# The product G v of a twelve-layer linear attention kernel: from one float32 product to three float32r passes of 128 columns

## The chip, the cores and the metric

The kernel runs on one core of a Trainium2 chip. The metric is the device time of one execution in microseconds. The engines are called as the profile calls them: PE is TensorE (PEld its weight loads), DVE is VectorE, ACT is ScalarE, POOL is GpSimd and SP is SyncE, which issues transfers here.

## What is computed

Twelve layers of attention without a softmax over 16 sequences of 256 tokens with 128 features, in 16 heads of 8 features, then a residual sum, a layer norm, a gated feed-forward network of 384 hidden features, and a second residual sum and layer norm. Cut to what matters:

```python
for i in range(12):
    qkv = x @ Wqkv[i].T + bqkv[i]
    q, k, v = jnp.split(qkv, 3, axis=-1)          # each (16, 256, 128), then split in 16 heads
    att = jnp.einsum('bhqd,bhkd->bhqk', q, k) * scale
    y = jnp.einsum('bhqk,bhkd->bhqd', att, v)
    x = y @ Wproj[i].T + bproj[i] + x
x = layernorm(x0 + x)
x = layernorm(x + ((silu(x @ wg.T) * (x @ wu.T)) @ wd.T))
```

## The kernel before

Since there is no softmax, q (k^T v) can be taken in any order, and the kernel never forms the tokens of the inner layers. It keeps for each sequence an affine map t (`tst`, 128 x 130: a 128 x 128 matrix and a column for the offset) that takes the tokens of the input to those of the layer. With the centred Gram matrix G of the input tokens, 128 x 128 for each sequence (`g0`), a layer needs per head only the small product k^T (G v), where k and v stand for the maps times the weights.

The 16 sequences are worked on in eight pairs (PB = 2), and the pairs in two sets of four (G = 4, NO = 2), half a layer apart. The steps of one layer are:

1. `products` for each pair. From the second layer on: k and v of both sequences into one PSUM bank by `mm_kv` (L439 to L441: three float32r passes of 256 columns a sequence, high and low halves of the map times high and low halves of the weights, without low times low), a copy of the bank's 512 columns to `kv` in SBUF, then q by `mm_q` (L447 to L449: three float32r passes of 260 columns a pair), its copy to the q part of `qgv`, and G v by `mm_gv` (L460: one float32 product of 128 columns for each sequence, from `g0` and the v part of `kv`), and its copy to the last part of `qgv`. In the first layer v is the raw weight itself, and k and q come from raw weights too.
2. `heads` for each set: the small products of k and G v of all heads by `mm_m` (L504), the sum with an offset term (L514) and a mask, then y by `mm_y` (L522).
3. `projection` for each pair: a high half of y (copy, ACT or DVE), a low half (subtraction on DVE, L535), three passes of 260 columns by `mm_w` (L539 to L541), the sum into `tst` (DVE, L546), and new halves of the map, `thl`: the high one on ACT (L204, a copy helper), the low one on POOL (L209, a subtraction helper).

Ahead of the layers, `prologue` makes the Gram matrices of a pair (L341) and takes off the mean on DVE, which writes `g0` (L358). Behind them, `ffn` works through the eight pairs; its pair p overlaps the last layer where there is room. Its high and low halves of the hidden features lie in tiles `hh0`, `hh1`, `hl0` and `hl1`, one group for each pair, 512 float32r columns each.

The order of instructions on each engine is written by a planner, `Plan`. Each operation has its costs on the engines that may do it, what it reads and writes, and a priority (the layer, plus half a layer for the second set, plus small amounts such as QLATE = 0.3 for q). `Plan.run` keeps a clock for each engine and takes again and again, among the operations that could start first, the one with the lowest priority number. Where an operation may run on ACT or DVE, the one that would end earlier gets it. The planner's clock is an estimate; on the chip the order alone stands, and semaphores make an engine wait. PSUM has eight banks, which the planner hands out (`Val("bank")`).

The planner's costs that bear on the change are the following:

```python
def mm32(n=C):
    return max(220, 4 * n / 2.4 + 8)
def mmr(n):
    return max(111, 0.447 * n + 5)
```

Of the kernel before, what the change touches and what calls it, by code (L numbers as in the profile page):

```python
# [9 lines left out]
F32 = mybir.dt.float32  # L10
F32R = mybir.dt.float32r
# [3 lines left out]
ALU = mybir.AluOpType  # L15
# [6 lines left out]
C = 128  # L22
# [3 lines left out]
PB = 2  # L26
NP = B // PB
# [6 lines left out]
NB = 2  # L34
# [38 lines left out]
PE, ACT, DVE, POOL, SP = "pe", "act", "dve", "pool", "sp"  # L73
# [92 lines left out]
# [8 lines that stand above are left out]
def act(n, sbuf=False, pointers=0):  # L174
    return (94 if sbuf else 51) + 93 * pointers + n / 1.2


def dve(n, fast=False):
    return 69 + n / (1.92 if fast else 0.96)


def pool(n):
    return 147 + 2.1 * n


def flat(t):
    return t.rearrange("p a b -> p (a b)")
# [3 lines left out]
def linear_attention_ffn_kernel(ctx: ExitStack, tc: tile.TileContext, x, xt, wall, wq0, bias, wg, wu, wd, out):  # L191
    nc = tc.nc
# [3 lines left out]
    new = lambda name, shape, dt=F32: sb.tile([128, *shape], dt, name=name)  # L196

    plan = Plan({"bank": 8, "raw": RAW, "weights": WSLOTS, "turned": WSLOTS})
    banks = [ps.tile([128, 512], F32, name=f"bank{i}") for i in range(8)]
    bank = lambda v: banks[v.slot]  # L200

    def copy(e, dst, src):
        if e == ACT:
            nc.scalar.copy(dst, src)  # L204
        else:
            (nc.vector if e == DVE else nc.gpsimd).tensor_copy(dst, src)  # L206
# [71 lines left out]
    wraw = [new(f"wraw{i}", [4 * C]) for i in range(RAW)]  # L278
# [40 lines left out]
    thl = [new(f"thl{p}", [2, PB, W], F32R) for p in range(NP)]  # L319
    means = new("means", [B])  # L320
    g0 = [new(f"g0_{p}", [PB, C]) for p in range(NP)]
    kvs = [new(f"kv{p}", [PB, 2, C]) for p in range(NP)]
    qss = [t[:, : PB * W].rearrange("p (a b) -> p a b", b=W) for t in qgvs]
    gvs = [t[:, PB * W :].rearrange("p (a b) -> p a b", b=C) for t in qgvs]
    yhl = [new(f"yhl{p}", [2, PB * W], F32R) for p in range(NP)]
    named = lambda: [Val() for _ in range(NP)]
    vt, vc, vhi, vlo, vm, vg0, vkv, vyh, vyl, vqo, vw = (named() for _ in range(11))

    nmeans, tmeans = new("nmeans", [B]), new("tmeans", [B])

# [92 lines left out]
    def products(l, p, prio):  # L423

        raw, whv, _ = wts[l]
        bs = slice(p * PB, (p + 1) * PB)
        hl = lambda i, s, n=1: whl[whv.slot][:, i, s * C : (s + n) * C]
        hi, lo = thl[p][:, 0], thl[p][:, 1]
        kv, qs, gv = kvs[p], qss[p], gvs[p]
        if l == 0:  # L430
            tv = lambda b: wraw[raw.slot][:, 2 * C : 3 * C]
            src = raw
        else:
            pkv, pq = Val("bank"), Val("bank")

            def mm_kv(e):
                for b in range(PB):
                    o = bank(pkv)[:, b * 2 * C : (b + 1) * 2 * C]
                    nc.tensor.matmul(o, hi[:, b, 0:C], hl(0, 1, 2), start=True, stop=False)  # L439
                    nc.tensor.matmul(o, hi[:, b, 0:C], hl(1, 1, 2), start=False, stop=False)  # L440
                    nc.tensor.matmul(o, lo[:, b, 0:C], hl(0, 1, 2), start=False, stop=True)  # L441
            plan.op({PE: 6 * mmr(256)}, mm_kv, [vhi[p], vlo[p], whv], [pkv], prio)
            plan.op({ACT: act(512), DVE: dve(512)}, lambda e: copy(e, kv.rearrange("p a b c -> p (a b c)"), bank(pkv)), [pkv], [vkv[p]], prio)

            def mm_q(e):
                o = bank(pq)[:, : PB * W]
                nc.tensor.matmul(o, hl(0, 0), flat(hi), start=True, stop=False)  # L447
                nc.tensor.matmul(o, hl(0, 0), flat(lo), start=False, stop=False)  # L448
                nc.tensor.matmul(o, hl(1, 0), flat(hi), start=False, stop=True)  # L449
            plan.op({PE: 3 * mmr(PB * W)}, mm_q, [vhi[p], vlo[p], whv], [pq], prio + QLATE)  # L450
            q = lambda: bank(pq)[:, : PB * W].rearrange("p (b w) -> p b w", w=W)
            plan.op({ACT: act(PB * C), DVE: dve(PB * C)}, lambda e: copy(e, qs[:, :, 0:C], q()[:, :, 0:C]), [pq], [vq[p]], prio + QLATE)
            plan.op({DVE: 130}, lambda e: nc.vector.tensor_scalar(qs[:, :, C], q()[:, :, C], bcol[:, l, 0:1], None, ALU.add), [pq, vbias], [vqo[p]], prio + QLATE)  # L453
            tv = lambda b: kv[:, b, 1, :]
            src = vkv[p]
        pgv = Val("bank")

        def mm_gv(e):
            for b in range(PB):
                nc.tensor.matmul(bank(pgv)[:, b * C : (b + 1) * C], g0[p][:, b, :], tv(b), start=True, stop=True)  # L460
        plan.op({PE: 2 * mm32()}, mm_gv, [vg0[p], src], [pgv], prio)
        plan.op({ACT: act(256), DVE: dve(256)}, lambda e: copy(e, flat(gv), bank(pgv)[:, : PB * C]), [pgv], [vgv[p]], prio)
        if l == L - 1:

            def rest(e):
                copy(e, tst[:, bs, 0:C], center.unsqueeze(1).to_broadcast([128, PB, C]))
                copy(e, tst[:, bs, C], mb[:, bs])
            plan.op({ACT: act(PB * C, True) + 100, DVE: dve(PB * C, True) + 75}, rest, [vhi[p], vlo[p], vmb], [vt[p], vc[p]], prio)
# [90 lines left out]
    for t in cps:  # L559
        nc.gpsimd.memset(t, 0.0)  # L560
    for p in range(NP):
        t = {f"{n}{j}": new(f"{n}{j}_{p}", [512], F32R) for n in ("hh", "hl") for j in range(NB)}
        t.update({
            "tt": qgvs[p][:, PB * W : PB * W + 2 * C], "x1": kvs[p].rearrange("p a b c -> p (a b c)"), "sg0": xts[p], "sg1": qgvs[p][:, :512],
            "xh": flat(yhl[p])[:, :512], "xl": thl[p].rearrange("p a b c -> p (a b c)")[:, :512],
            "ve": new(f"ve{p}", [4]), "rs": new(f"rs{p}", [4]), "nb": new(f"nb{p}", [4]), "nm": new(f"nm{p}", [4]), "st": new(f"st{p}", [K, 3]),
            "cr": new(f"crow{p}", [PB]), "cp": cps[p % 2], "cq": cqs[p % 2],
        })
        ctxs.append(t)
# [147 lines left out]
    for l in range(L):  # L717
        if l + 1 < L:
            prep_weights(l + 1)
        for o in range(NO):  # L720
            at = l + OSTEP * o
            for p in range(o * G, (o + 1) * G):
                products(l, p, at)
            for r, py in enumerate(heads(l, o, at, [(l, o)] * (l < OWN) + [(l + o, 1 - o)] * (OWN <= l + o < L))):
                projection(l, o * G + r, py, at + (LSTEP * r if l == L - 1 else 0))
        if l < NP:
            center_tokens(l, l + 2)
# [35 lines left out]
```

## Time and profile before

| what | value |
|---|---|
| median of three runs | 309.67 us (308.54 to 309.88) |
| time of the profiled execution | 309.26 us |
| span of the profiled execution, first to last instruction | 307.2 us |
| PE, PEld busy | 297.3 us (97%), 272.3 us (89%) |
| DVE, ACT, POOL busy | 227.2 (74%), 221.3 (72%), 136.4 us (44%) |
| mean granted TensorE clock | 0.989 |
| G v, layers two to twelve | 352 instructions for 176 products, from 27.8 to about 236 us |

The busy time of an engine is the union of its instructions' times. TensorE's matmuls are pipelined: one starts well before the one ahead of it has ended, so what each takes of the engine is read from the distance between starts, and not from its length. A float32 product of TensorE appears as two instructions, each with a weight load, and a float32r pass as one with one load. The shapes of float32r operands are shown as f32 in TensorE's rows.

### The profile page before, as it was taken

The page shows a single profiled execution, that of the slowest core. Times are in us where ns is not written, and L with a number is a line of the kernel's source. Part 1 is how long each engine was busy: PE and PEld are TensorE (multiplying, and loading weights), DVE is VectorE, ACT ScalarE, POOL GpSimd, SP SyncE. Part 2 cuts the span into 40 slices and gives each one's busy share as a digit, 9 for nine tenths or more (in the row PEclk, how much of TensorE's full clock was granted, in tenths as well). Part 3 has the DMA queues.
Part 4 walks back from the last instruction along what each step waited for, and adds up shares of the span by engine and source line. Part 5 has one row for each costly group of instructions (what it writes and reads, how often), then busy time and mean ns, then how long its engine had stood idle before and what let it go on. Part 6 is the DMA issues. An engine that isn't in the chain of part 4 may idle for free.

```text
span 307.2 us, 12904 instructions
## 1 busy us (share of the span) xinstructions
PE 297.3 (97%) x5384; PEld 272.3 (89%) x5384; DVE 227.2 (74%) x680; ACT 221.3 (72%) x571; POOL 136.4 (44%) x234
## 2 busy tenths in 40 slices
PE   8999999999999999999999999999999999999971
PEld 8989999999999999999999999999999988888840
DVE  3797887777677676776767877787554699899993
ACT  2547877867768677777677666776986768968964
POOL 6246353334541345314453144521442456568582
PEclk9999999999999999999999999999999999999995
DMA  7534213122031120311202112130000000000214
GB/s 211 149 99 128 71 39 89 35 55 71 9 82 38 42 84 2 90 37 43 82 4 53 38 28 55 30 81 2 4 2 3 2 1 2 0 0 22 83 34 137
DMA packets 22489, 15.65 MB, mean 51 GB/s; under 512 B 1952, under 2 KB 19872, under 8 KB 22432
## 3 DMA queue, kind: packets, MB, share of 16 engines
q1 hardware_dynamic: 21872, 14.62, 17.5%
q8 instruction: 42, 0.69, 0.9%
q10 hardware_dynamic: 560, 0.22, 0.3%
q14 instruction: 15, 0.12, 0.1%
HBM read 8.02 MB, written 2.10 MB: 33 GB/s over the span
## 4 chain that ended last, share of the span: by engine, by line
PE 88%; DVE 7%; ACT 3%; issue 1%; POOLq 0%; POOL 0%
PE bank L460 14%; PE bank L439 8%; PE bank L522 8%; PE bank L441 7%; PE bank L440 7%; PE bank L447 5%; PE bank L504 5%; PE bank L541 4%; PE bank L539 4%; PE bank L540 4%; PE bank L448 3%; PE bank L449 3%; PE bank L341 3%; PE bank L665 2%; PE bank L681 2%; PE bank L682 2%
## 5 line engine op out<-in xcount | busy, mean ns | idle before, releaser
L209 POOL TENSOR_TENSOR thl<-tst,thl 128x260 fp32r<-128x260 f32 x88 | 64.5, 764 | 122.9 <-ACT thl L204 122.9
L204 ACT COPY qgv<-bank 128x256 f32<-128x256 f32 x171 | 60.8, 376 | 20.5 <-PE bank L449 13.5
L204 ACT COPY kv<-bank 128x512 f32<-128x512 f32 (+1 forms) x93 | 53.3, 575 | 18.6 <-PE bank L441 13.4
L439 PE MATMUL bank<-whl,thl 128*128 128x256 f32 x176 | 51.8, 294 | 0.0
L441 PE MATMUL bank<-whl,thl 128*128 128x256 f32 x176 | 49.6, 282 | 0.0
L440 PE MATMUL bank<-whl,thl 128*128 128x256 f32 x176 | 49.4, 281 | 0.0
L460 PE MATMUL bank<-kv,g 128*128 128x128 f32 x352 | 46.0, 275 | 0.0
L546 DVE TENSOR_TENSOR tst<-bank,tst 128x260 f32<-128x260 f32 x96 | 36.9, 425 | 11.9 <-PE bank L541 9.1
L204 ACT CAST thl<-tst 128x260 fp32r<-128x260 f32 x88 | 33.0, 408 | 14.6 <-DVE tst L546 14.5
L460 PEld LDWEIGHTS bank<-kv,g 128*128 128x128 f32 x352 | 42.7, 191 | 0.4 <-issue 0.4
L453 DVE TENSOR_SCALAR qgv<-bank,bcol 128x2 f32<-128x2 f32 x88 | 19.3, 221 | 27.6 <-ACT qgv L204 23.0
L439 PEld LDWEIGHTS bank<-whl,thl 128*128 128x128 f32 x176 | 33.1, 188 | 4.1 <-issue 4.0
L535 DVE TENSOR_TENSOR yhl<-bank,yhl 128x260 fp32r<-128x260 f32 x96 | 34.3, 421 | 2.4 <-ACT yhl L204 2.4
L440 PEld LDWEIGHTS bank<-whl,thl 128*128 128x128 f32 x176 | 33.2, 189 | 0.0
L441 PEld LDWEIGHTS bank<-whl,thl 128*128 128x128 f32 x176 | 33.1, 188 | 0.0
L447 PE MATMUL bank<-thl,whl 128*128 128x260 f32 x88 | 29.0, 329 | 0.0
L522 PE MATMUL bank<-qgv,gm 32*32 32x130 f32 x1536 | 25.9, 280 | 0.2 <-DVE gm L212 0.2
L204 ACT CAST yhl<-bank 128x260 fp32r<-128x260 f32 (+1 forms) x61 | 22.3, 418 | 5.2 <-PE bank L522 3.8
L206 DVE CAST yhl<-bank 128x260 fp32r<-128x260 f32 x43 | 16.5, 424 | 11.8 <-PE bank L522 11.8
L448 PE MATMUL bank<-thl,whl 128*128 128x260 f32 x88 | 24.8, 282 | 0.0
L449 PE MATMUL bank<-thl,whl 128*128 128x260 f32 x88 | 24.7, 281 | 0.0
L522 PEld LDWEIGHTS bank<-qgv,gm 32*32 32x32 f32 x1536 | 17.3, 103 | 5.6 <-ACT kv L204 0.3
(153 smaller groups left out, 705.8 us busy)
## 6 DMA issues: line engine op xcount, KB each, us to landing
wraw<-wall SPq DMA_DIRECT2D x12, 256.0 KB, 3.0
wpt<-whl SPq DMA_DIRECT2D x24, 96.0 KB, 2.2
qgv<-x SPq DMA_DIRECT2D x8, 256.0 KB, 5.4
xt<-xt SPq DMA_DIRECT2D x8, 256.0 KB, 3.3
out<-kv SPq DMA_DIRECT2D x7, 256.0 KB, 2.3
wpt<-whl SPq DMA_DIRECT2D x24, 64.0 KB, 2.6
wpt<-whl SPq DMA_DIRECT2D x24, 32.0 KB, 1.9
wraw<-wg SPq DMA_DIRECT2D x1, 192.0 KB, 3.4
```

The source lines that it names most:

```text
L204: nc.scalar.copy(dst, src)
L209: (nc.vector if e == DVE else nc.gpsimd).tensor_tensor(dst, a, b, ALU.subtract)
L439: nc.tensor.matmul(o, hi[:, b, 0:C], hl(0, 1, 2), start=True, stop=False)
L440: nc.tensor.matmul(o, hi[:, b, 0:C], hl(1, 1, 2), start=False, stop=False)
L441: nc.tensor.matmul(o, lo[:, b, 0:C], hl(0, 1, 2), start=False, stop=True)
L447: nc.tensor.matmul(o, hl(0, 0), flat(hi), start=True, stop=False)
L448: nc.tensor.matmul(o, hl(0, 0), flat(lo), start=False, stop=False)
L449: nc.tensor.matmul(o, hl(1, 0), flat(hi), start=False, stop=True)
L460: nc.tensor.matmul(bank(pgv)[:, b * C : (b + 1) * C], g0[p][:, b, :], tv(b), start=True, stop=True)
L522: nc.tensor.matmul(bank(pys[r])[group(g + r), b * W : (b + 1) * W], gm[group(g), r * PB + b, :], qss[p][group(g), b, :], start=True, stop= ...
L535: plan.op({DVE: dve(PB * W)}, lambda e: nc.vector.tensor_tensor(yl, bank(py)[:, : PB * W], yh.bitcast(F32), ALU.subtract), [py, vyh[p]], [ ...
L546: plan.op({DVE: dve(PB * W)}, lambda e: nc.vector.tensor_tensor(ts, bank(pw)[:, : PB * W], ts, ALU.add), [pw], [vt[p], vc[p]], prio)
```

## The change

From the second layer on, `mm_gv` computes G v of each sequence in three float32r passes of 128 columns that add up in PSUM: high G times high v, high G times low v, low G times high v. The first layer keeps its float32 product.

The halves of G are made once for each pair, on POOL, in the first layer (a rounding copy and a subtraction). They lie in the tiles `hh0` and `hl0` of the feed-forward stage: the high and low half of G in `hh0`, those of v in `hl0`. These tiles are now allocated ahead of the layers.

The one copy of k and v out of PSUM (128 x 512) becomes three operations on 128 x 256: the high half of v (a rounding copy, ACT or DVE), the low half of v (a subtraction, on DVE alone), and the copy of k (ACT or DVE). The v part of `kv` is not written any more from the second layer on. The cost that the planner takes for `mm_gv` stays 2 * mm32().

```diff
+    hhl = [{f"{n}{j}": new(f"{n}{j}_{p}", [512], F32R) for n in ("hh", "hl") for j in range(NB)} for p in range(NP)]
+    ghl, vhl = ([t[n].rearrange("p (i b c) -> p i b c", b=PB, c=C) for t in hhl] for n in ("hh0", "hl0"))
...
-            plan.op({ACT: act(512), DVE: dve(512)}, lambda e: copy(e, kv.rearrange("p a b c -> p (a b c)"), bank(pkv)), [pkv], [vkv[p]], prio)
+            half = lambda s: bank(pkv).rearrange("p (b s c) -> p b s c", s=2, c=C)[:, :, s, :]
+            vh, vl = vhl[p][:, 0], vhl[p][:, 1]
+            plan.op({ACT: act(256), DVE: dve(256)}, lambda e: copy(e, vh, half(1)), [pkv], [vvh[p]], prio)
+            plan.op({DVE: dve(256)}, lambda e: nc.vector.tensor_tensor(vl, half(1), vh.bitcast(F32), ALU.subtract), [pkv, vvh[p]], [vvl[p]], prio)
+            plan.op({ACT: act(256), DVE: dve(256)}, lambda e: copy(e, kv[:, :, 0, :], half(0)), [pkv], [vkv[p]], prio)
...
-            tv = lambda b: kv[:, b, 1, :]
-            src = vkv[p]
         pgv = Val("bank")
 
         def mm_gv(e):
             for b in range(PB):
-                nc.tensor.matmul(bank(pgv)[:, b * C : (b + 1) * C], g0[p][:, b, :], tv(b), start=True, stop=True)
-        plan.op({PE: 2 * mm32()}, mm_gv, [vg0[p], src], [pgv], prio)
+                o = bank(pgv)[:, b * C : (b + 1) * C]
+                if l == 0:
+                    nc.tensor.matmul(o, g0[p][:, b, :], wraw[raw.slot][:, 2 * C : 3 * C], start=True, stop=True)
+                else:
+                    gh, gl, vh, vl = ghl[p][:, 0, b], ghl[p][:, 1, b], vhl[p][:, 0, b], vhl[p][:, 1, b]
+                    nc.tensor.matmul(o, gh, vh, start=True, stop=False)
+                    nc.tensor.matmul(o, gh, vl, start=False, stop=False)
+                    nc.tensor.matmul(o, gl, vh, start=False, stop=True)
+        plan.op({PE: 2 * mm32()}, mm_gv, [vg0[p], src] if l == 0 else [vgh[p], vvh[p], vvl[p]], [pgv], prio)
         plan.op({ACT: act(256), DVE: dve(256)}, lambda e: copy(e, flat(gv), bank(pgv)[:, : PB * C]), [pgv], [vgv[p]], prio)
+        if l == 0:
+            def halves(e):
+                nc.gpsimd.tensor_copy(flat(ghl[p][:, 0]), flat(g0[p]))
+                nc.gpsimd.tensor_tensor(flat(ghl[p][:, 1]), flat(g0[p]), flat(ghl[p][:, 0]).bitcast(F32), ALU.subtract)
+            plan.op({POOL: 2 * pool(256)}, halves, [vg0[p]], [vgh[p]], prio + 0.4)
```

More of the change, by code (lines that the diff above doesn't have):

```diff
@@ L326, in linear_attention_ffn_kernel @@
     named = lambda: [Val() for _ in range(NP)]
-    vt, vc, vhi, vlo, vm, vg0, vkv, vyh, vyl, vqo, vw = (named() for _ in range(11))
+    vt, vc, vhi, vlo, vm, vg0, vkv, vyh, vyl, vqo, vw, vgh, vvh, vvl = (named() for _ in range(14))
     nmeans, tmeans = new("nmeans", [B]), new("tmeans", [B])
@@ L430, in products @@
         if l == 0:
-            tv = lambda b: wraw[raw.slot][:, 2 * C : 3 * C]
             src = raw
@@ L561, in linear_attention_ffn_kernel @@
     for p in range(NP):
-        t = {f"{n}{j}": new(f"{n}{j}_{p}", [512], F32R) for n in ("hh", "hl") for j in range(NB)}
+        t = dict(hhl[p])
         t.update({
```

## The prediction

> **What bounds the kernel now.** I read the page's first two parts, then the chain of waits, then a table of twenty-microsecond windows over the layers, and last the order of single instructions on TensorE. The busy shares and the chain come first:
>
> ```profile
> PE 297.3 (97%) x5384; PEld 272.3 (89%) x5384; DVE 227.2 (74%) x680; ACT 221.3 (72%) x571; POOL 136.4 (44%) x234
> PE 88%; DVE 7%; ACT 3%; issue 1%; POOLq 0%; POOL 0%
> PE bank L460 14%; PE bank L439 8%; PE bank L522 8%; PE bank L441 7%; PE bank L440 7%; PE bank L447 5%; PE bank L504 5%; PE bank L541 4%; PE bank L539 4%; PE bank L540 4%; PE bank L448 3%; PE bank L449 3%; PE bank L341 3%; PE bank L665 2%; PE bank L681 2%; PE bank L682 2%
> ```
>
> The chain that ended last runs on TensorE for 88% of the span, and the matmul of the change, L460, is its largest line: 14% of 307.2 us, some 43 us. Two windows from the middle of the layers say the same (columns: window, its length, then busy us of PE, PEld, DVE, ACT, POOL, clock, DMA):
>
> ```profile
> 90.00:110.00 20.00, 20.00 (x423) 18.78 (x422) 14.37 (x44) 14.84 (x39) 7.98 (x12) 1.00 0.19 53
> 110.00:130.00 20.00, 20.00 (x433) 18.65 (x436) 14.23 (x44) 14.84 (x40) 7.98 (x12) 1.00 0.19 49
> ```
>
> TensorE has no gap, at a granted clock of 1.00; VectorE and ScalarE have a quarter of their time free. So from about 24 us to 290 us time is what TensorE issues, and whatever lengthens or shortens its stream moves the end one for one. Since pipelined matmuls overlap, a busy time of "275 ns" is no price; the price is the distance between starts. That comes from the order of instructions:
>
> ```profile
> 151.13 0.28 PE L440 MATMUL bank<-whl,thl 128*128 128x256 f32 x1
> 151.25 0.28 PE L441 MATMUL bank<-whl,thl 128*128 128x256 f32 x1
> 151.37 0.28 PE L439 MATMUL bank<-whl,thl 128*128 128x256 f32 x1
> 156.47 1.43 PEld L460 LDWEIGHTS bank<-kv,g 128*128 128x128 f32 x12
> 156.59 1.50 PE L460 MATMUL bank<-kv,g 128*128 128x128 f32 x12
> 18.01 0.30 PEld L416 LDWEIGHTS bank<-mb,center 128*128 128x128 f32 x2
> 18.11 0.29 PE L416 MATMUL bank<-mb,center 128*128 128x16 f32 x2
> 236.38 0.28 PE L657 MATMUL bank<-identb,cp 128*128 128x128 bf16 x2
> ```
>
> A float32r pass of 256 columns starts 0.12 us after the one before. Twelve float32 instructions of L460 take 1.50 us with the last one's 0.275: (1.50 - 0.275) / 11 = 0.1114 us apart. There are 352 of them for 176 products (11 layers, 16 batches), so one product of float32 is two instructions, 0.223 us, and a pair of batches is four, 0.446 us. The rows of L416 tell what sets that distance: with only 16 columns to stream, the two weight loads still start (0.30 - 0.19) / 1 = 0.11 us apart. Streaming cannot take that long for 16 columns; the load of 128 weight columns does. Its length agrees with this:
>
> ```profile
> L460 PEld LDWEIGHTS bank<-kv,g 128*128 128x128 f32 x352 | 42.7, 191 | 0.4 <-issue 0.4
> L440 PEld LDWEIGHTS bank<-whl,thl 128*128 128x128 f32 x176 | 33.2, 189 | 0.0
> L504 PEld LDWEIGHTS bank<-qgv,kv 128*32 128x32 f32 x1408 | 14.8, 109 | 0.2 <-issue 0.2
> L657 PEld LDWEIGHTS <-cp 128*128 128x128 bf16 x16 | 1.3, 98 | 0.4 <-issue 0.3
> ```
>
> From 32 to 128 weight columns a float32 load grows from 109 to 191 ns, 0.85 ns a column, so 128 columns are 0.109 us. A float32r load (L440, weights of thl) lasts 189 ns like a float32 one, not 98 like the bf16 one. And L439 and L440, which have the same weights one after the other, show 176 loads each: a load is not skipped when the weights repeat.
>
> **The change part by part.** *The passes.* Removed for each pair from the second layer on: 4 float32 instructions, 4 x 0.1114 = 0.446 us. Added: 2 batches x 3 float32r passes, 6 loads of 128 columns and 6 streams of 128 columns. The trace holds no float32r pass under 256 columns, so I bound its distance. Below: 0.061 us, from bf16 passes of 128 columns in L657, (0.28 - 0.219) / 1. Above: a whole float32 product, 0.223 us, if a narrow float32r pass streams no faster than float32. I take 0.111 us, since the float32r load has the float32 load's length, and every row with such a load (L416, L460) has that distance even with next to nothing to stream; halving 256 columns of 0.12 us gets the stream under the load, which then sets the pace. So 6 x 0.111 = 0.666 us, 0.220 more for a pair, and 88 pairs (11 layers x 8) make 88 x 0.220 = +19.4 us. All of it is on the path, since the windows show no gap to put it in. The matmul stays behind the same operations of the queue, so all of TensorE's later work moves with it.
>
> The Trainium skill sees this twice, and more kindly. "TensorE: Matmul & The Clock Gate", section "Back-to-back issue gap", gives about 81 ns for each load and matmul of 128 columns in a sustained stream; the sum by it would be an estimated +3.5 us, and the 111 ns of L460's rows speak against it here. "FP8 and Floating Point Precision", section "TensorE Precision Notes", counts four passes for true float32; by that count alone, three instead of four save a quarter of L460's time, an estimate of 10 us less; the trace has two loads where that page has four passes, and three loads are more than two.
>
> *The copies out of PSUM.* Removed: one copy of 128x512, 587 ns on ScalarE. Added: the upper half of v (128x256, 376 ns by the row of the qgv copies), the k copy (376 ns), and on VectorE alone the lower half of v, a subtraction from PSUM like L535's 421 ns. That is 586 ns more for a pair, 51.6 us in all, spread over two engines. In the ten windows from 30 to 230 us VectorE and ScalarE are busy 145.4 and 148.7 us, 294 of 400; with 48 us more in a stretch of about 218 us each it is 342 of 437, 78% instead of 74%. If every copy stays on ScalarE, VectorE comes to 83% and ScalarE to 74%. Neither takes TensorE's place. What hides them is TensorE's own work on the other pairs of the set: its q passes (3 x 0.121 us a pair, 1.45 us for four) and the other set's k and v.
>
> *The longer wait.* G v now waits for two steps (376 + 421 ns, and a hand-over of some 0.1 us between the engines) instead of one of 587: 0.31 us more. If the wait stands at TensorE's head, everything behind it waits too: the next set's q, k and v and the projection. The subtraction itself waits on VectorE behind the upper half; behind it are the subtraction of y's halves and the sum into tst. It costs nothing as long as other matmuls can go first, which the operation order written by the planner allows; exposed once in each half layer it would be 22 x 0.31 = 6.8 us. A gain from copying k later is not to be had, since k is needed only by the per-head products after G v. I take 1 us.
>
> *The halves of G.* Eight times on POOL, in the first layer: a cast and a subtraction of 128x256, each near the 731 ns of POOL's gm product, 1.5 us a pair, 12 us in all. POOL has 4.6 + 1.5 + 3.1 + 4.6 us of work in the first 31 us by the page's slices, so there is room for it; but a step of 1.5 us may stand ahead of the subtraction for the next layer's thl, which starts at 23.0 us and is waited for. Between 0 and 1.5 us; I take 0.5. No DMA, and nothing on SP, is added; the tiles used are those of the later feed-forward stage.
>
> *Sum.* 309.26 (the profiled execution: span 307.2 and 2.1 around it) + 19.4 + 1 + 0.5 = 330.2; the median of the runs shown is 0.4 above the profiled one, hence 330.5 us.
>
> **The rivals.** *Passes go at streaming pace* (ends faster). If the float32r load with 128 columns can hide wholly, as bf16's does, a pass costs 0.061 us: 6 x 0.061 = 0.366, 0.080 less a pair, 7.0 us less, 303.5 us with the 1 us and 0.5 us left in. It is decided at 0.446 / 6 = 0.074 us a pass: below that the change gains, above it loses. For it: fewer part products than float32. Against it: float32r's load rows of 189 ns. Between this and the forecast lies a pass of 0.085, half way from 0.061 to 0.109: 6 x 0.085 = 0.510, +5.6 us, 315 us.
>
> *Narrow float32r streams as slowly as float32.* No row of this trace excludes it. 6 x 0.223 = 1.338 us a pair, 0.892 more, +78.5 us: 389 us. Against it: at 256, 260 and 512 columns the distances (0.12, 0.12, 0.23 us) lie on one line of about 0.43 ns a column, with no sign of a step on the way down.
>
> *The wait for v's lower half stands open* beside the passes: 309.7 + 19.4 + 6.8 + 1.5 = 337 us, up to 344 if VectorE's queue is a further 0.3 us late each time (22 x 0.3 = 6.6). For it: VectorE becomes the busier of the two helpers. Against it: a fifth of it is still free.
>
> *The change doesn't do what it says*, that is, narrow passes are compiled into the same two float32 instructions each: then the price is that of the second rival, and it is counted there.
>
> **How the numbers follow.** The forecast, load-bound passes with little exposed, has 0.72 (324 to 337 us). The exposed wait has 0.06, slow narrow streams 0.12, streaming pace or between 0.10: of that 0.07 is faster, 0.01 the same, 0.02 slower. A measurement of this kernel tells about 0.5% (1.5 us) from no change. So slower is 0.72 + 0.06 + 0.12 + 0.02 = 0.92. The range from 315 (the pass of 0.085 us) to 344 (the exposed wait at its worst) holds 0.72 + 0.06 + 0.02 = 0.80; the slow streams above and the gain below are what is left out.
>
> **What would show each step.** Right: the G v line of layers from the second on has 528 matmuls instead of 352, of float32r, at 0.11 us from start to start, with 528 loads of about 190 ns; its share of the chain rises to some 19%; the layers' windows still show TensorE at 20.00 of 20 and VectorE near 16; a layer takes 1.8 us more, and the part after the layers has its old length. Wrong in the first step: starts 0.06 to 0.08 us apart, or 0.2. Wrong in the second: gaps on TensorE released by VectorE's lower half of v. Wrong in the third: the first k and v matmuls of the second layer later than 23.65 us by more than 1.5 us. If TensorE shows gaps of over 10 us in all in the layers, the reasoning that only its stream counts was wrong.

## The result and the profile after

The changed kernel takes 332.05 us, median of 4 runs (331.52 to 332.34), against 309.75 us for the kernel before. The ratio is 1.0728, with a 95% interval from 1.0703 to 1.0753: 22.5 us slower (21.8 to 23.3). The forecast was 330.5 us, and the time lies in its range. The profiled execution took 332.34 us, with a span of 330.6 us at a granted clock of 0.986.

The page after, parts 1, 4 and 5 (G v is now L469 to L471; k and v are L441 to L443; L538 is y):

```profile
PE 316.9 (96%) x5560; PEld 290.7 (88%) x5560; DVE 263.2 (80%) x790; ACT 225.0 (68%) x638; POOL 146.0 (44%) x249
PE 84%; DVE 8%; ACT 3%; issue 2%; DMA 2%; SPq 0%; POOL 0%; POOLq 0%; DVEq 0%
PE bank L441 8%; PE bank L538 7%; PE bank L443 6%; PE bank L442 6%; PE bank L471 6%; PE bank L470 6%; PE bank L469 6%; PE bank L520 4%; PE bank L453 4%; PE bank L555 4%; PE bank L557 3%; PE bank L556 3%; PE bank L454 3%; PE bank L455 3%; PE bank L681 2%
L471 PE MATMUL bank<-hl,hh 128*128 128x128 f32 x176 | 48.4, 275 | 0.0
L471 PEld LDWEIGHTS bank<-hl,hh 128*128 128x128 f32 x176 | 33.8, 192 | 0.0
L448 DVE TENSOR_TENSOR hl<-bank,hl 128x256 fp32r<-128x256 f32 x88 | 36.8, 420 | 5.8 <-ACT kv L204 5.4
```

TensorE still carries the chain. It has 176 more matmuls and 176 more weight loads; a load lasts 192 ns, as a float32 load did. G v's three lines have 18% of the chain together, where the one line had 14%. The lower half of v costs DVE 36.8 us, and DVE's share rises from 74% to 80%. The windows of twenty microseconds in the middle of the layers:

```profile
90.00:110.00 20.00, 19.99 (x423) 18.71 (x422) 16.81 (x51) 13.24 (x40) 6.25 (x9) 1.00 0.18 49
110.00:130.00 20.00, 19.98 (x423) 18.70 (x423) 16.46 (x52) 13.04 (x39) 6.26 (x10) 1.00 0.19 49
```

TensorE is as full as before, VectorE is at 16.5 to 16.8 of 20, and ScalarE has become a little freer. The order of instructions on TensorE around one pair's G v gives the distance between starts, in the first column:

```profile
150.96 0.28 PE L557 MATMUL bank<-yhl,wpt 128*128 128x260 f32 x1
151.08 0.22 PE L469 MATMUL bank<-hl,hh 128*128 128x128 f32 x1
151.13 0.28 PE L470 MATMUL bank<-hl,hh 128*128 128x128 f32 x1
151.25 0.27 PE L471 MATMUL bank<-hl,hh 128*128 128x128 f32 x1
151.36 0.27 PE L469 MATMUL bank<-hl,hh 128*128 128x128 f32 x1
151.47 0.27 PE L470 MATMUL bank<-hl,hh 128*128 128x128 f32 x1
151.58 0.28 PE L471 MATMUL bank<-hl,hh 128*128 128x128 f32 x1
151.69 0.33 PE L453 MATMUL bank<-thl,whl 128*128 128x260 f32 x1
151.87 0.28 PE L454 MATMUL bank<-thl,whl 128*128 128x260 f32 x1
```

Inside the block, starts stand 0.11 us apart. The first gap is 0.05 us, and the gap behind L453 is 0.18 in the place of 0.12, which gives it back. The weight loads of the same stretch, the first three and the one behind the block shown, start 0.11 to 0.12 us apart all through. L469 begins 0.12 us behind the start of its load, as the wide passes do, and L470 only 0.05 us:

```profile
150.96 0.19 PEld L469 LDWEIGHTS bank<-hl,hh 128*128 128x128 f32 x1
151.08 0.19 PEld L470 LDWEIGHTS bank<-hl,hh 128*128 128x128 f32 x1
151.19 0.19 PEld L471 LDWEIGHTS bank<-hl,hh 128*128 128x128 f32 x1
...
151.63 0.19 PEld L453 LDWEIGHTS bank<-thl,whl 128*128 128x128 f32 x1
```

From 151.08 to 151.87 it is 0.79 us: six times 0.11 and one wide pass of 0.12.

A good clock for where time goes is the start of the y products (L522 before, L538 after), one block for each half layer. The table gives how much later than in the kernel before each kernel's blocks start, in us, and the drift for a layer between the 6th and the 22nd block, eight layers apart. Its lower rows belong to the experiments.

| kernel | 1st block | 2nd | 6th | 22nd | 24th, the last | drift a layer |
|---|---|---|---|---|---|---|
| before, start at | 19.07 | 26.81 | 64.52 | 220.55 | 243.46 | |
| after | +1.20 | +2.70 | +7.98 | +22.57 | +22.83 | +1.82 |
| halves_alone | +1.28 | +1.33 | +1.29 | +1.62 | +1.63 | +0.04 |
| copies_alone | -0.52 | +1.82 | +3.62 | +3.89 | +2.36 | +0.03 |
| one_copy | +1.36 | +1.41 | +5.02 | +19.28 | +21.06 | +1.78 |
| two_passes | +0.68 | +2.17 | +3.84 | +4.14 | +2.61 | +0.04 |
| wide | +1.64 | +3.13 | +5.01 | +5.98 | +4.27 | +0.12 |
| three_wide | +0.52 | +2.02 | +7.88 | +25.26 | +25.83 | +2.17 |
| bf16_halves | +0.64 | +1.95 | +3.07 | +0.24 | -2.08 | -0.35 |
| copies_late | -0.56 | -0.28 | -0.32 | +0.39 | -0.42 | +0.09 |
| bf16_late | -0.36 | -0.36 | -0.23 | -3.66 | -5.12 | -0.43 |
| halves_sub | -0.23 | +0.62 | +0.78 | +0.62 | +0.60 | -0.02 |

The drift of the changed kernel, 1.82 us a layer, is 0.228 us a pair; the prediction had 0.220. Beside it there is a loss in the first three layers that the prediction had put at 1.5 us.

The clock also moves when the order on TensorE changes. In the changed kernel 12 more k and v passes than before, 1.4 us, stand ahead of both the 6th and the 22nd block, and none ahead of the 24th; the same holds for copies_alone and two_passes. So the last column is the one to hold against the times, and of the 7.98 us at the 6th block 1.4 are order and some 3.6 the passes of 16 pairs, which leaves 3 us of loss.

### The profile page after: what moved, and what is told of

It reads as the page before. It is cut to its first block, busy times and chain, and to the rows that moved or that the text cites. A ratio compares the mean times of both kernels' runs of the same rounds, so it can differ in the third digit from the quotient of the medians.

```text
span 330.6 us, 13508 instructions
## 1 busy us (share of the span) xinstructions
PE 316.9 (96%) x5560; PEld 290.7 (88%) x5560; DVE 263.2 (80%) x790; ACT 225.0 (68%) x638; POOL 146.0 (44%) x249
## 4 chain that ended last, share of the span: by engine, by line
PE 84%; DVE 8%; ACT 3%; issue 2%; DMA 2%; SPq 0%; POOL 0%; POOLq 0%; DVEq 0%
PE bank L441 8%; PE bank L538 7%; PE bank L443 6%; PE bank L442 6%; PE bank L471 6%; PE bank L470 6%; PE bank L469 6%; PE bank L520 4%; PE bank L453 4%; PE bank L555 4%; PE bank L557 3%; PE bank L556 3%; PE bank L454 3%; PE bank L455 3%; PE bank L681 2%
## 5 line engine op out<-in xcount | busy, mean ns | idle before, releaser
L204 ACT COPY qgv<-bank 128x256 f32<-128x256 f32 x175 | 64.4, 377 | 26.1 <-PE bank L471 17.2
L441 PE MATMUL bank<-whl,thl 128*128 128x256 f32 x176 | 52.5, 298 | 0.0
L204 ACT CAST hl<-bank 128x256 fp32r<-128x256 f32 x82 | 30.9, 377 | 28.3 <-PE bank L443 26.3
L562 DVE TENSOR_TENSOR tst<-bank,tst 128x260 f32<-128x260 f32 x96 | 36.8, 426 | 16.4 <-PE bank L557 12.5
L443 PE MATMUL bank<-whl,thl 128*128 128x256 f32 x176 | 49.5, 281 | 0.0
L471 PE MATMUL bank<-hl,hh 128*128 128x128 f32 x176 | 48.4, 275 | 0.0
L470 PE MATMUL bank<-hl,hh 128*128 128x128 f32 x176 | 48.4, 275 | 0.0
L469 PE MATMUL bank<-hl,hh 128*128 128x128 f32 x176 | 47.2, 268 | 0.0
L448 DVE TENSOR_TENSOR hl<-bank,hl 128x256 fp32r<-128x256 f32 x88 | 36.8, 420 | 5.8 <-ACT kv L204 5.4
L441 PEld LDWEIGHTS bank<-whl,thl 128*128 128x128 f32 x176 | 33.1, 188 | 3.0 <-issue 2.2
L469 PEld LDWEIGHTS bank<-hl,hh 128*128 128x128 f32 x176 | 33.6, 191 | 2.2 <-issue 1.8
L471 PEld LDWEIGHTS bank<-hl,hh 128*128 128x128 f32 x176 | 33.8, 192 | 0.0
L470 PEld LDWEIGHTS bank<-hl,hh 128*128 128x128 f32 x176 | 33.7, 191 | 0.0
L443 PEld LDWEIGHTS bank<-whl,thl 128*128 128x128 f32 x176 | 33.1, 188 | 0.1
L459 DVE TENSOR_SCALAR qgv<-bank,bcol 128x2 f32<-128x2 f32 x88 | 18.2, 217 | 14.4 <-ACT qgv L204 9.5
L204 ACT COPY kv<-bank 128x256 f32<-128x256 f32 x71 | 27.1, 382 | 2.8 <-DVE hl L206 2.6
```

The costliest lines, as they stand in the source:

```text
L448: plan.op({DVE: dve(256)}, lambda e: nc.vector.tensor_tensor(vl, half(1), vh.bitcast(F32), ALU.subtract), [pkv, vvh[p]], [vvl[p]], prio)
L469: nc.tensor.matmul(o, gh, vh, start=True, stop=False)
L470: nc.tensor.matmul(o, gh, vl, start=False, stop=False)
L471: nc.tensor.matmul(o, gl, vh, start=False, stop=True)
L562: plan.op({DVE: dve(PB * W)}, lambda e: nc.vector.tensor_tensor(ts, bank(pw)[:, : PB * W], ts, ALU.add), [pw], [vt[p], vc[p]], prio)
```

## The experiments

The theory: a float32r pass of 128 columns costs its weight load, 0.111 us, and two more loads a pair make the time. Rival one: the split copies and the longer wait make a good part of it. Rival two: columns streamed are the price, or a fixed price of any pass.

### The parts one by one

**halves_alone** is the kernel before with the operation that makes the halves, and nobody reads them:

```diff
+        if l == 0:
+            def halves(e):
+                nc.gpsimd.tensor_copy(flat(ghl[p][:, 0]), flat(g0[p]))
+                nc.gpsimd.tensor_tensor(flat(ghl[p][:, 1]), flat(g0[p]), flat(ghl[p][:, 0]).bitcast(F32), ALU.subtract)
+            plan.op({POOL: 2 * pool(256)}, halves, [vg0[p]], [vgh[p]], prio + 0.4)
```

> The kernel before, with the halves of G made on POOL in the first layer and read by nobody. If they delay the start of the second layer, as the profile after suggests (its first k and v matmul came 1.1 us later), the time is 310.8 to 312.8 us, 1 to 3 above the kernel before. If the loss in the first layers belongs to the copies and the wait for v's low half, it stays within 0.5 us of 309.75.

Measured: 310.2 us, ratio 1.0044 (1.0028 to 1.0061), 1.4 us. It is nearly all there at the first block (+1.28, and +1.63 at the last).

**copies_alone** is the kernel before with the split copies and the wait:

```diff
-            plan.op({ACT: act(512), DVE: dve(512)}, lambda e: copy(e, kv.rearrange("p a b c -> p (a b c)"), bank(pkv)), [pkv], [vkv[p]], prio)
...
+            plan.op({ACT: act(256), DVE: dve(256)}, lambda e: copy(e, kv[:, :, 1, :], half(1)), [pkv], [vvh[p]], prio)
+            plan.op({DVE: dve(256)}, lambda e: nc.vector.tensor_tensor(vl, half(1), kv[:, :, 1, :], ALU.subtract), [pkv, vvh[p]], [vvl[p]], prio)
+            plan.op({ACT: act(256), DVE: dve(256)}, lambda e: copy(e, kv[:, :, 0, :], half(0)), [pkv], [vkv[p]], prio)
...
-        plan.op({PE: 2 * mm32()}, mm_gv, [vg0[p], src], [pgv], prio)
+        plan.op({PE: 2 * mm32()}, mm_gv, [vg0[p], src] if l == 0 else [vg0[p], vvh[p], vvl[p]], [pgv], prio)
```

> The kernel before with its float32 product, but v copied alone, a subtraction on DVE that writes a tile nobody multiplies, k copied alone, and G v made to wait for the subtraction. If weight loads make the change's time, this adds 0 to 2 us: 309.8 to 312. If the longer wait at TensorE's head carries a good part of the 22 us, it adds 7 us or more: 317 and up.

Measured: ratio 1.0076 (1.0047 to 1.0105), 2.35 us, 311.74 us: a little over the theory's upper end by the ratio, and far from the rival's 7. By the table the loss arises by the third layer, and from there on the copies cost nothing: the drift is 0.03 us a layer. (That the first block comes 0.5 us earlier here than in the kernel before was not traced.) In the second layer DVE's order shows where the larger part comes from. First the kernel before, then this one:

```profile
24.31 0.47 DVE L212 TENSOR_TENSOR kvo<-vbb,kb 128x256 f32<-128x256 f32 x1
24.88 0.42 DVE L514 TENSOR_TENSOR gm<-bank,kvo 128x256 f32<-128x256 f32 x1
25.34 1.03 DVE L212 TENSOR_TENSOR gm<-gm,mask 128x256 f32<-128x256 f32 x1
```

```profile
24.23 0.44 DVE L401 STREAM_TRANSPOSE vbb<-vb 128x256 f32<-128x256 f32 x1
25.40 0.42 DVE L206 COPY kv<-bank 128x256 f32<-128x256 f32 x1 [0.74 <-ACT kv L204]
25.74 0.83 DVE L212 TENSOR_TENSOR kvo<-vbb,kb 128x256 f32<-128x256 f32 x1
26.50 0.41 DVE L448 TENSOR_TENSOR hl<-bank,kv 128x256 fp32r<-128x256 f32 x1
26.83 0.41 DVE L520 TENSOR_TENSOR gm<-bank,kvo 128x256 f32<-128x256 f32 x1
27.16 0.41 DVE L448 TENSOR_TENSOR hl<-bank,kv 128x256 fp32r<-128x256 f32 x1
27.49 0.99 DVE L212 TENSOR_TENSOR gm<-gm,mask 128x256 f32<-128x256 f32 x1
```

A copy of the split stands at the head of DVE's queue and waits 0.74 us for ScalarE; the offset product kvo and the sum into gm stand behind it, and two subtractions come between. gm is ready at 28.5 us in the place of 26.4. TensorE then waits 1.10 us for it, in the order of TensorE's instructions:

```profile
28.63 1.06 PE L528 MATMUL bank<-qgv,gm 32*32 32x130 f32 x64 [1.10 <-DVE gm L212]
```

In the third layer it waits once more, 0.81 us for a VectorE step on q:

```profile
54.55 0.28 PE L387 MATMUL bank<-tst,wraw 128*32 128x8 f32 x13 [0.81 <-DVE qgv L459]
```

**one_copy** has the passes and the halves, but not the split copies; the second pass takes high v in the place of low v:

```diff
-            plan.op({ACT: act(256), DVE: dve(256)}, lambda e: copy(e, vh, half(1)), [pkv], [vvh[p]], prio)
-            plan.op({DVE: dve(256)}, lambda e: nc.vector.tensor_tensor(vl, half(1), vh.bitcast(F32), ALU.subtract), [pkv, vvh[p]], [vvl[p]], prio)
-            plan.op({ACT: act(256), DVE: dve(256)}, lambda e: copy(e, kv[:, :, 0, :], half(0)), [pkv], [vkv[p]], prio)
+            plan.op({ACT: act(512), DVE: dve(512)}, lambda e: copy(e, hhl[p]["hl0"], bank(pkv)), [pkv], [vkv[p]], prio)
...
-                    nc.tensor.matmul(o, gh, vl, start=False, stop=False)
+                    nc.tensor.matmul(o, gh, vh, start=False, stop=False)
```

> The kernel after, but k and v leave PSUM in one rounding copy of 512 columns as before, and the second pass takes high v in the place of low v (v's low half is left out of the product). Loads as the cause: still six passes a pair, 329 to 331.5 us. Copies and waiting as a large part: 325 us or less.

Measured: 330.48 us, ratio 1.0685 (1.0665 to 1.0705), 21.2 us. Without any of the new copies and waits the loss is nearly whole, and the drift is 1.78 us a layer, 0.223 a pair. Rival one falls.

**two_passes** is the other way round: all copies and waits, and as many loads as the float32 product had.

```diff
-                    nc.tensor.matmul(o, gh, vl, start=False, stop=False)
```

> The kernel after without the pass of high G times low v (that term is left out), all copies and waits kept: four loads a pair, as many as the float32 product had. At 0.111 us a pass 2 x 88 x 0.111 = 19.5 us come off 332.05: 312.5 us. If a pass costs less at the margin because waiting would fill its place, 318 us or more.

Measured: 312.41 us, ratio 1.0112 (1.0083 to 1.0141), with a drift of 0.04 us a layer. By the ratios 0.0616 x 309.2 = 19.0 us come off, and by the drifts (1.82 - 0.04) / 16 = 0.111 us a pass. What is left, 3.5 us, is near the halves and the copies together (1.4 + 2.35).

### Loads, columns, or passes

**wide** streams the same columns with one load less:

```diff
-                    nc.tensor.matmul(o, gh, vh, start=True, stop=False)
-                    nc.tensor.matmul(o, gh, vl, start=False, stop=False)
-                    nc.tensor.matmul(o, gl, vh, start=False, stop=True)
+                    o = bank(pgv)[:, 2 * b * C : 2 * (b + 1) * C]
+                    nc.tensor.matmul(o, gh, vhl[p][:, :, b], start=True, stop=False)
+                    nc.tensor.matmul(o[:, 0:C], gl, vh, start=False, stop=True)
...
+            plan.op({ACT: act(256), DVE: dve(256)}, lambda e: copy(e, gv, part(0)), [pgv], [vgv[p]], prio)
+            plan.op({DVE: dve(256)}, lambda e: nc.vector.tensor_tensor(gv, part(1), gv, ALU.add), [pgv], [vgv[p]], prio)
```

> The kernel after with the two passes of high G joined: one pass moves high and low v side by side (256 columns), low G times high v is added to its first half, and the two halves are summed on DVE on the way out of PSUM. The same 384 columns are streamed for a sequence as in the change, with two loads in the place of three. Loads as the price: a pair takes 2 x (0.12 + 0.111) = 0.462 us in the place of 0.666, 88 x 0.204 = 18 us off 332, 314 us, plus up to 3 us for the sum on DVE. Columns as the price: no more than 3 us off, 329 us or more.

Measured: 313.78 us, ratio 1.0149 (1.0132 to 1.0167). The drift, 0.12 us a layer or 0.015 a pair, is what 0.462 against 0.446 gives. DVE has 19.2 of 20 us busy in its windows by the sum it gained, and even that costs only the first layers.

**three_wide** keeps three loads and doubles the columns:

```diff
+                    o, both = bank(pgv)[:, 2 * b * C : 2 * (b + 1) * C], vhl[p][:, :, b]
+                    nc.tensor.matmul(o, gh, both, start=True, stop=False)
+                    nc.tensor.matmul(o, gh, both, start=False, stop=False)
+                    nc.tensor.matmul(o, gl, both, start=False, stop=True)
...
```

> The kernel after, each of its three passes twice as wide: high and low v side by side, 256 columns, high G taken twice; only the first half of the sum is copied out (it leaves low v out of the product and doubles the high term). Three loads as in the change, twice the columns. Loads as the price: 6 x (0.12 - 0.111) = 0.05 us more a pair, 88 x 0.05 = 5 us, 337 us at most. Columns as the price: a pass of 0.111 becomes 0.222, 58 us more, 390 us.

Measured: 335.7 us, ratio 1.0862 (1.0842 to 1.0881), 4.1 us above the changed kernel by the ratios. Twice the columns cost 4 us where one load fewer gave 18: at this width columns are nearly free.

**bf16_halves** keeps three passes and the copies, and makes the loads shorter. The halves of G lie in G's own place, those of v in the v part of kv:

```diff
+            vh, vl = (kv[:, :, 1, 64 * i : 64 * i + 64].bitcast(BF16) for i in range(2))
...
+                    gh, gl, vh, vl = (t[:, 64 * i : 64 * i + 64].bitcast(BF16) for t in (g0[p][:, b], kv[:, b, 1]) for i in range(2))
...
+            plan.op({ACT: act(512, True), DVE: dve(512)}, lambda e: copy(e, g0[p].bitcast(BF16), kv[:, :, 1, :].bitcast(BF16)), [vgh[p], vkv[p]], [vg0[p]], prio + 0.4)
```

> The kernel after with halves in bf16 (16 bits of G and v kept in all, in two parts), the same three passes and copies, and one more copy of G's halves for each pair in the first layer. A bf16 load is 98 ns long in the profile before, and two bf16 passes of 128 columns stood 0.061 us apart. Loads as the price: 6 x 0.061 = 0.366 us a pair, 88 x 0.300 = 26.4 us off 332, 306 us, below the kernel before. A fixed price of a pass whatever its load: 330 us or more.

Measured: 307.14 us, ratio 0.9938 (0.9915 to 0.996): below the kernel before, with the same three passes that made the change slower. Rival two falls in both its forms: neither the columns nor a fixed price of any pass makes the time. That it is the load of a float32r pass, and no other price that every float32r pass would have, these runs don't separate, since load and pass come one with one. For the load speak its length (192 ns against 98) and two kinds of float32 rows of the kernel before: with 128 weight columns and 16 to stream (L416) the loads started 0.11 us apart, while 24 passes with 32 weight columns and 8 to stream were through in 0.21 us, from their first start to that of the next line:

```profile
22.63 0.38 PE L385 MATMUL bank<-tst,wraw 128*32 128x8 f32 x24
22.84 0.88 PE L504 MATMUL bank<-qgv,wraw 128*32 128x32 f32 x64
```

The order of instructions on TensorE in bf16_halves shows the passes (L467 to L469) and what is not won:

```profile
120.69 0.23 PE L467 MATMUL bank<-kv,g 128*128 128x128 bf16 x1
120.75 0.22 PE L468 MATMUL bank<-kv,g 128*128 128x128 bf16 x1
120.81 0.22 PE L469 MATMUL bank<-kv,g 128*128 128x128 bf16 x1
120.86 0.22 PE L467 MATMUL bank<-kv,g 128*128 128x128 bf16 x1
120.92 0.22 PE L468 MATMUL bank<-kv,g 128*128 128x128 bf16 x1
120.97 0.22 PE L469 MATMUL bank<-kv,g 128*128 128x128 bf16 x1
121.00 0.36 PE L451 MATMUL bank<-thl,whl 128*128 128x260 f32 x1
121.21 0.28 PE L452 MATMUL bank<-thl,whl 128*128 128x260 f32 x1
```

Six passes take 0.31 us, but the float32r pass behind them takes 0.21 in the place of 0.12, 0.09 more: 0.40 a pair. This is paid once for each block of G v, and the block shown holds one pair. A block of two (at 97.73 us) takes 0.74 us by the same reckoning and one of four (at 87.99 us) 1.41, or 0.37 and 0.35 a pair, so that between 0.05 and 0.09 a pair is won. With the steady layers' mix of such blocks a layer should win some 0.6 us by estimate, as bf16_late does below, and the drift is -0.35. A part of the difference is waiting: from 65 to 221 us TensorE waits 0.8 us in all for VectorE's sum into tst. The rest was not traced.

### The loss in the first layers

**halves_mb** asks whether one held step is the price of the halves. In halves_alone, around the first sum into gm (its order of instructions):

```profile
17.22 1.27 POOL L209 TENSOR_TENSOR whl<-wraw,whl 128x512 fp32r<-128x512 f32 x1
...
17.27 1.29 DVE L417 TENSOR_SCALAR mb<-means,bcol 128x16 f32<-128x16 f32 x1
...
18.43 0.41 DVE L521 TENSOR_TENSOR gm<-bank,kvo 128x256 f32<-128x256 f32 x1
```

In the kernel before the same step and the sum behind it:

```profile
17.53 0.23 DVE L415 TENSOR_SCALAR mb<-means,bcol 128x16 f32<-128x16 f32 x1
...
17.67 0.42 DVE L514 TENSOR_TENSOR gm<-bank,kvo 128x256 f32<-128x256 f32 x1
```

A step of 16 columns lasts 1.06 us longer beside a POOL subtraction that used to come later.

```diff
-        plan.op({DVE: 133}, lambda e: nc.vector.tensor_scalar(mb, means, bcol[:, L - 1, 3:4], None, ALU.add), [vbias, *vm], [vmb], prio)
+        plan.op({ACT: 220}, lambda e: nc.scalar.activation(mb, means, AF.Identity, bias=bcol[:, L - 1, 3:4]), [vbias, *vm], [vmb], prio)
```

> The kernel before with the halves of G on POOL, and the last layer's offset sum (mb, 128x16 from SBUF to SBUF) on ACT in the place of DVE. In the run with the halves alone this DVE step lasted 1.29 us in the place of 0.23, all of it beside POOL's subtraction for whl, with the sum into gm behind it on DVE. If that hold is the halves' price, the first block of y products starts within 0.4 us of the kernel before (19.1 to 19.5 us) and the time is within 0.5 us of it. If the price is POOL's time for the halves themselves, the 1.3 us stay.

Measured: 311.09 us, ratio 1.0051 (1.0031 to 1.0072), first block 1.23 us late. It missed. The hold had only moved to the next DVE step from SBUF to SBUF, a copy of two columns, while POOL ran the same subtraction (16.64 to 18.11 us):

```profile
16.64 1.47 POOL L209 TENSOR_TENSOR whl<-wraw,whl 128x512 fp32r<-128x512 f32 x1
...
16.96 1.21 DVE L349 COPY tst<-means 128x2 f32<-128x2 f32 x1
```

**halves_sub** therefore takes the POOL subtraction away from there. It is put back behind the last g0, and the second set's halves behind the first gm:

```diff
-        after = [vlo[G - 1]] if l > 1 else []
+        after = [vlo[G - 1]] if l > 1 else [vg0[NP - 1]] if l else []
...
-            plan.op({POOL: 2 * pool(256)}, halves, [vg0[p]], [vgh[p]], prio + 0.4)
+            plan.op({POOL: 2 * pool(256)}, halves, [vg0[p], *([vgm[0]] if p >= G else [])], [vgh[p]], prio + 0.4)
```

> The kernel with the halves of G alone, with POOL's queue kept as before ahead of the first mask product: the weights' subtraction for the second layer waits for the last g0, and the halves of the second set of pairs wait for the first gm. In the runs with the halves alone the weights' subtraction had come forward on POOL, from 19.5 to 17.2 us, and a DVE step from SBUF to SBUF stood beside it for 1.1 us longer than alone, ahead of the sum into gm. If that is the price of the halves, the first block of y products starts within 0.5 us of 19.07 and the time is within 0.7 us of the kernel before; if the halves cost by POOL's own time, 1.3 us or more stay.

Measured: 309.75 us, ratio 1.0023 (1.0006 to 1.0039), 0.7 us. The first block starts at 18.84 us, mb lasts 0.23 us again, and the same halves are still made on POOL. So the loss at the first block was the hold; in the changed kernel too mb lasts 1.28 us. By the times alone little can be said, since the two intervals overlap. What is left in this kernel comes between the first block and the second, from -0.23 to +0.62. The order on POOL and on TensorE shows it:

```profile
22.23 0.40 POOL L467 CAST hh<-g 128x256 fp32r<-128x256 f32 x1
22.71 0.74 POOL L468 TENSOR_TENSOR hh<-g,hh 128x256 fp32r<-128x256 f32 x1
23.41 3.29 POOL L209 TENSOR_TENSOR thl<-tst,thl 128x260 fp32r<-128x260 f32 x4
...
23.53 0.28 PE L442 MATMUL bank<-whl,thl 128*128 128x256 f32 x1
24.20 0.39 PE L443 MATMUL bank<-whl,thl 128*128 128x256 f32 x1 [0.40 <-POOL thl L209]
```

The halves of one pair stand directly ahead of thl's subtraction, which starts at 23.41 us and not at 23.04, and TensorE waits 0.40 us for it. That is the delay that the prediction had named, and the order of this kernel has it.

The Trainium skill's page "SBUF — State Buffer", section "SBUF: two separate sides", has a rule for such rows: VectorE and GpSimd share a pair of ports under an exclusive lock, which the one that starts first holds for its whole instruction; on VectorE's side it names two-port modes and steps with two inputs from SBUF. The two held rows agree with the lock, since they end at 18.56 and 18.17 us, 0.07 and 0.06 us behind POOL's subtraction. Whether these steps are of the kinds named, no row tells.

**copies_late** begins the split copies in the fourth layer only (`if l < 3` keeps the one copy and its product).

> The kernel with the copies alone, but with the one copy of 512 columns in the second and third layer; the split copies and the wait for the subtraction begin in the fourth layer. If their price is an ordering of DVE's queue in the first layers, where copies wait ahead of the sum into gm, the time is within 0.7 us of the kernel before. If it is paid wherever they begin, the 2.4 us stay.

Measured: 308.7 us, ratio 0.9988 (0.9973 to 1.0004). The 2.35 us are gone. The copies have a price in the first layers alone. (The 22nd block has six more k and v passes ahead of it than in the kernel before, 0.7 us, which is all of the drift of 0.09.)

**bf16_late** joins what was found: bf16 halves, made after the third layer's product and used from the fourth layer on.

```diff
-                if l == 0:
-                    nc.tensor.matmul(o, g0[p][:, b, :], wraw[raw.slot][:, 2 * C : 3 * C], start=True, stop=True)
+                if l < 3:
+                    nc.tensor.matmul(o, g0[p][:, b, :], kv[:, b, 1, :] if l else wraw[raw.slot][:, 2 * C : 3 * C], start=True, stop=True)
...
-        if l == 0:
+        if l == 2:
             def halves(e):
```

> The kernel with bf16 halves, begun in the fourth layer: the halves of G are made after the third layer's product, and the second and third layer keep their float32 product and one copy. 72 pairs gain 0.080 us by the load's price, 5.8 us, and the first layers' 3.8 us are not paid: 303.5 to 304.5 us. If the first layers' loss only moves with the change, 306 to 308 us.

Measured: 304.06 us, ratio 0.9834 (0.981 to 0.9857), the fastest kernel here, 5.1 us below the one before. From the 8th block, which starts 0.03 us earlier than before, to the 24th it wins 5.1 us in eight layers, 0.080 us a pair as expected; the drift in the table is smaller, because it takes in the layer of the change-over, in which nothing is won, and since six more k and v passes stand ahead of the 22nd block. It keeps some 16 bits of G and v in this product, fewer than float32 or two float32r halves.

## Why the prediction was right, point by point

*The bound.* Right. TensorE's stream sets the end: passes added or taken away moved the time by what their distances say, in both directions, and copies on other engines did not once the layers were running.

*The price of a pass.* Right: 0.111 us taken, 0.111 measured by the drifts of the changed kernel and two_passes. That columns do not set it is shown by wide and three_wide, and that it is no fixed price of any pass by bf16_halves; that it is the load is the best reading of these and of L416's 16 columns, with the reserve made at bf16_halves. The term of 19.4 us came out as 19.0. The prediction drew two more sums from the Trainium skill, and the trace has neither: not the +3.5 us by "TensorE: Matmul & The Clock Gate", section "Back-to-back issue gap", nor the 10 us less by "FP8 and Floating Point Precision", section "TensorE Precision Notes". Float32r passes of 128 columns stood 0.11 us apart.

*The copies and the wait.* Sized too small, and put in the wrong place: 1 us taken, 2.35 measured for the copies alone. The prediction looked for G v's wait at TensorE's head, spread over the half layers, and named y's halves and the sum into tst as what stands behind on VectorE. In the runs it was a wait at DVE's head in the second layer, with kvo and gm behind it and 1.10 us of waiting on TensorE, and in the third layer 0.81 us for a step on q. A stall in the steady layers, 0.31 us for each of 22 half layers, did not come.

*The halves of G.* Also sized too small: 0.5 us taken, 1.4 measured, and by another way than the one named. Not a half ahead of thl's subtraction, which in halves_alone waited 0.27 us for ScalarE itself, but POOL's other work coming forward and holding a DVE step. The way named did come in halves_sub, where the hold was gone: 0.40 us. The first k and v matmul of the second layer came at 24.73 us, 1.1 us late, within the 1.5 that the prediction gave as the bound.

*The sum.* 20.9 us were forecast and 22.5 measured; the gap of 1.6 us is in these two terms, 3.75 us measured alone where 1.5 were taken. Alone, the parts add up to 19.0 + 1.4 + 2.35 = 22.75 us, within the interval of the measured 22.5.

*The signposts* came as written: 528 loads of 190 ns, starts 0.11 us apart, full windows, 1.8 us a layer, and VectorE near 16 of 20. G v's share of the chain is 18% where 19% was written.

## What to carry to other kernels

Price a matmul by the distance between starts in rows of its own shape, and find out which side sets it by a row where the other side is nearly nothing; here 16 columns cost as much as 128. Splitting a float32 product in three passes pays only if a pass is shorter than two thirds of the float32 instruction, so count weight loads before part products, and look for a cheaper load before a cheaper stream. Work handed to an idle engine can still cost its neighbours at the start of a kernel, where the queues have no slack; the start of one block a layer, compared between two traces, tells such a loss from one that grows with the layers, as long as the same work stands ahead of the block in both.

## What the runs showed of the hardware

A float32r weight load of 128 columns is as long as a float32 one (192 and 191 ns against 98 for bf16), and in a row of such passes the loads start 0.11 us apart and the passes too, except the second behind a wide pass (0.05 us). A wide float32r pass behind a block of bf16 passes takes 0.21 us to the next start in the place of 0.12, once for each block. A DVE step of 2 or 16 columns from SBUF to SBUF took 1.21 and 1.29 us while POOL subtracted 512 columns, against 0.16 and 0.23 in runs where POOL was not doing so.
